# Two parts of a scan layer, instead of one and a half, computed between the experts of the layer before

## The chip, the cores and the metric

The kernel runs on one core of a Trainium2 chip. The metric is device time in microseconds (us) of one execution: the median of several runs. Engines are named as in the profile: PE (TensorE matmul) and PEld (its weight loads), DVE (VectorE), ACT (ScalarE), POOL (GpSimd), SP (SyncE, which here only issues DMAs).

## What is computed

Two transformer layers on x of 16 x 256 x 128 (batch, tokens, features) in float32, each with an attention-like half and a feed-forward half; both halves have a layer norm with a shift and a scale before them and a gate after them.

Layer 0: attention with 16 heads, then 16 experts (gate and up 128 to 256, down 128 to 128), all of them computed for every token and weighted by the scores of the router's best four. Layer 1: first the part that this change concerns,

```
k_real, v = x @ Wk, x @ Wv                    # 1024 columns: 16 heads of 64
k = exp(1j * 10 * k_real);  rotors = exp(1j * t * freqs)
out_pos   = real(cumsum_t(v * rotors)          * conj(rotors)) / sqrt(t + 1)
out_assoc = real(cumsum_t(v * conj(k_shifted)) * k)            / sqrt(t + 1)
y = (out_pos * g_pos + out_assoc * g_assoc) @ Wo
```

and then a small feed-forward half of three 128 x 128 matrices, called the mix below. With real numbers each cumulative sum is a cosine and a sine half (index `s`); `k` in the code is the batch element within a pair.

## The kernel before

The batch is taken in eight chunks (`NCH`) of two batch elements. Three stages follow one another, each with its instructions in an order written out by hand: on each engine they run in the order in which the program issues them.

**Attention of layer 0**, until about 302 us: not touched.

**The experts of layer 0**, about 302 to 690 us. The loop runs over n = 16 * chunk + e, so a step is one expert on one chunk. In a step PE makes three 128 x 512 products of two passes each: gate `pg` (L808) and up `pup` (L810) for n, and down into `acc` (L833) for n - 3. DVE adds bias to the gate (`g`, L812) and forms `u` for n - 1 (L824); ACT does `u` and the silu (L814, L817); POOL clamps `u` (L818) and multiplies it by the scores (`wide`, L825). Other work of a chunk is laid into fixed steps: the end of the old chunk at e = 2 to 4, the figures of the next layer norm on ACT at 5 and 6, its spread on POOL at 7 (L228, L229), the turning of the scores at 7. Generators that are advanced by one `next` per step put in more: `last_end` (router of the last chunk), `prepare` (the weights and rotors of layer 1, then `first_steps`), and `parts_ahead`.

`parts_ahead(c)` is what the change is about. The 1024 columns of the scan layer are eight parts j of 128 (`NJ`). For the first six chunks (`AHEAD` = 6) some of this is computed here, ahead of time, since layer 1 of a chunk can begin as soon as its layer 0 is through. It starts at e = 8 of the following chunk and computes, for chunk c, part 7 wholly (both sums) and of part 6 the position sum only. The work comes in pieces of 128 x 256, one for each (part, sum, k, s): POOL multiplies the values by the rotor or phasor (`bind`, L957), and in the next step DVE scans the product (L961), multiplies it by gate and probe (L965) and adds it to the total (L967), unless it is the first of its total. There are 12 pieces for a chunk, in steps 1 to 16 except 4, 7, 11 and 16. The two totals go to DRAM (L1007). Values and keys come from PE (L944, L979), their phases and sines from DVE (L985) and ACT (L983 to L989). PSUM pool `p_m` has one buffer for all of these.

**The scan layer and the mix**, from about 690 us. `PARTS` is the number of parts left for this stage: 7 for each of the first six chunks, 8 for the last two, so 58 steps. Part 6 of each of the first six chunks (`is_half`) has only its second sum to do here. In step n:

- DVE: scan of the assoc sum (`sum_assoc`, L1238) and of the position sum (`mem`, L1238), phases of n + 2 (`off`, L1213), `m_pos` (L1450), then parts of the mix and of the residual stream.
- POOL: read-out of the assoc sum of n - 1 (`sum_assoc`, L1456), then the two products to be scanned in n + 1 (`bound_pos`, `bound_assoc`, L1235).
- PE: assoc read-out of n - 1 into `pout` (L1252), mix matmuls, keys and values of n + 3 (L1197, L1201), position read-out of n (L1252).
- ACT: two sines and an absolute value for n + 2 (L1219 to L1221), the copies of keys and values out of PSUM (L1198, L1202), then parts of the mix.

A half step has one scan of two halves, one bound product, a read-out of which DVE takes one half (L1448) and POOL the other, and no `m_pos`.

`pout` has one PSUM buffer, so the first position read-out of a chunk waits until ACT's `gated_out` (L1277, oT) has read the old chunk's sum. The totals computed ahead are fetched at j = 1 (L1264) and enter `pout` by one matmul each (L1268): part 7 at j = 3, part 6 in the half step. The mix of chunk m is laid out by `place`, the number of steps since chunk m + 1 began, so that it spans the following chunks: means at 2, figures at 3, spread (POOL) at 4, norm at 5, `mix_tokens` at 6, the matmuls at 7, 8 and 9, the gating at 10 and 11, the output of the two batch elements at 12 and 13. With seven steps to a chunk, place 6 falls on the last step j = 6 and place 7 on j = 0 of the next chunk.

Of the kernel before, what the change touches and what calls it, by code (L numbers as in the profile page):

```python
# [11 lines left out]
F32 = mybir.dt.float32  # L12
# [6 lines left out]
P = 128  # L19
# [23 lines left out]

PARTS = [NJ - 1 if c < AHEAD else NJ for c in range(NCH)]
# [11 lines left out]
def tile_adaln_two_layers(ctx: ExitStack, tc: tile.TileContext, a: dict, out: bass.AP):  # L56
# [206 lines left out]
    with ExitStack() as moe_scope:  # L263
# [523 lines left out]
        with ExitStack() as scope:  # L787
# [141 lines left out]
            def parts_ahead(c):  # L929

# [7 lines left out]

                def values(j):
                    v = cross.tile([P, 2, T], F32, tag="o", name=f"v_ahead_{c}_{j}")
                    pv = p_m.tile([P, 2, T], F32, tag="m", name=f"pv0_{c}_{j}")
                    nc.tensor.matmul(pv, w_v1[:, ts(j, P)], flat, start=True, stop=True)  # L944
                    nc.scalar.copy(v, pv)
                    return v

                yield
                vs = {j: values(j)}
# [5 lines left out]
                def bind(q, nm, k, s, by):  # L955
                    t = cross.tile([P, T], F32, tag=("heads", "y")[s], name=f"bound_ahead_{nm}_{c}_{q}_{k}_{s}")
                    nc.gpsimd.tensor_tensor(t, vs[q][:, k, :], by, ALU.mult)  # L957
                    bound[q, nm, k, s] = t

                def read(q, nm, k, s, i, probe):  # L960
# [3 lines left out]
                    gate = gates[:, q, i : i + 1]  # L964
                    nc.vector.scalar_tensor_tensor(row if more else dst, row, gate, probe, ALU.mult, ALU.mult)  # L965
                    if more:
                        nc.vector.tensor_tensor(dst, row, dst, ALU.add)  # L967
                    written.add((q, k))

                cs = late.tile([P, 2, 2, T + 1], F32, tag="phasor_ahead", name=f"phasor_ahead_{c}")  # L970
                nc.gpsimd.memset(cs[:, :, :, 0:1], 0.0)
                assoc = [(j, "assoc", k, s, 1, cs[:, s, k, 0:T], cs[:, s, k, 1:]) for k in range(2) for s in range(2)]
                pos_, pos_before = (
                    [(q, "pos", k, s, 0, rotor[:, q, s, :], rotor[:, q, s, :]) for k in range(2) for s in range(2)]
                    for q in (j, j - 1)
                )
                yield
                pk = p_m.tile([P, 2, T], F32, tag="m", name=f"pk0_{c}")
                nc.tensor.matmul(pk, w_k1[:, ts(j, P)], flat, start=True, stop=True)  # L979
                off, size = (  # L980
                    cross.tile([P, 2, T], F32, tag="hn4", name=f"{nm}_ahead_{c}") for nm in ("off", "size")
                )
                nc.scalar.activation(off, pk, AF.Copy, bias=ROUND)  # L983
                yield
                nc.vector.scalar_tensor_tensor(off, off, ROUND, pk, ALU.subtract, ALU.subtract)  # L985
                nc.scalar.activation(size, off, AF.Abs)
                nc.scalar.activation(cs[:, 1, :, 1:], off, AF.Sin, scale=-TWO_PI_IN)
                yield
                nc.scalar.activation(cs[:, 0, :, 1:], size, AF.Sin, bias=half_pi, scale=-TWO_PI_IN)  # L989
                yield  # L990

                pieces = assoc + pos_ + pos_before
                late_one = None
                for step in range(1, NE + 1):
                    yield
                    if late_one:
                        read(*late_one[:5], late_one[6])
                        late_one = None
                    if step == 5:
                        vs[j - 1] = values(j - 1)  # L1000

                    if step not in (4, 7, 11, NE):
                        late_one = pieces.pop(0)
                        bind(*late_one[:4], late_one[5])
                assert not pieces and not late_one
# [3 lines left out]
            def past_others(steps=1):  # L1009

                while any((at["step"] + i) % NE in (3, 5, 7, *range(10, 16)) for i in range(steps)):
                    yield
# [154 lines left out]
    with ExitStack() as scope:  # L1167
# [55 lines left out]
        def is_half(n):  # L1223

            return steps[n][0] < AHEAD and steps[n][1] == NJ - 2

# [3 lines left out]
        def binders(n):  # L1230
            w = work[n]
            v2 = w["v"].unsqueeze(1).to_broadcast(both)
            for nm, bind in (("pos", rot(n)), ("assoc", phasor[n % 3][:, :, :, 0:T]))[is_half(n) :]:
# [3 lines left out]
        def summed(n, nm, dst, half=slice(0, 2)):  # L1237
            nc.vector.tensor_tensor_scan(  # L1238
                dst[:, half].rearrange("p s k t -> p (s k t)"),
                keep.rearrange("p (s k) t -> p s k t", k=2)[:, half].rearrange("p s k t -> p (s k t)"),  # L1240
                work[n][nm][:, half].rearrange("p s k t -> p (s k t)"),
# [176 lines left out]
        for n in range(last + 2):  # L1418
# [3 lines left out]
            place = {n - begin[m + 1]: m for m in (c - 2, c - 1) if 0 <= m < NCH - 1 and n <= last}  # L1422
# [5 lines left out]
            if j == 4 and AHEAD <= c + 1 < NCH:  # L1428
                into_tokens(c + 1, pt_tokens)
            if n <= last:  # L1430
                half = is_half(n)
                mem = p_mem.tile(both, F32, tag="mem", name=f"mem_{n}")
                if not half:
                    m_pos = hp.tile(both, F32, tag="m_pos", name=f"m_pos_{n}")
                m_assoc = hp.tile(both, F32, tag="sum_assoc", name=f"sum_assoc_{n}", bufs=3)
                work[n]["m"] = m_assoc
                if half:

                    summed(n, "assoc", mem, slice(0, 1))
                    summed(n, "assoc", m_assoc, slice(1, 2))  # L1440
                elif n:
# [217 lines left out]
```

## Time and profile before

| | us |
|---|---|
| median of 3 runs | 1080.41 |
| lowest, highest | 1078.15, 1080.94 |
| the profiled execution's own time | 1078.81 |
| its span (first to last instruction) | 1076.7 |

| stage | about, us | steps |
|---|---|---|
| attention of layer 0 | 0 to 302 | |
| experts of layer 0 | 302 to 690 | 128 |
| scan layer and mix | 690 to 1053, end of the last chunk to 1074 | 58 |

The granted TensorE clock is at full speed in all 40 slices of the page. A line of a stretch gives its bounds and length in us, then the busy time (and the number of instructions) of PE, PEld, DVE, ACT and POOL, then granted clock, busy share of the DMA engines and GB/s. A line of a timeline gives start and duration, engine, source line, operation, what is written and read, and in brackets how long the engine had stood idle and for what. A line of a group gives in addition the number of instructions, their busy time and the mean duration in ns. Durations overlap the next instruction's by some 0.05 us, so a sum of times goes by starts. Matmuls show 0.59 us each but start 0.43 us apart.

### The profile page before, as it was taken

Reading aid. Unit: us, or ns where it says so; the run is one execution under the profiler, and the core shown is the slowest. Engines: PE = TensorE matmul, PEld = TensorE weight load, DVE = VectorE, ACT = ScalarE, POOL = GpSimd, SP = SyncE. Lnnn points to the kernel's source line nnn. Section 1 sums busy time; section 2 is a strip of 40 time slices with the busy share of each in tenths; the row PEclk is TensorE's granted clock in tenths of the full one; section 3 lists DMA queues with packets and bytes.
Section 4 is the critical chain, followed back from the end, with each engine's and each line's share of the span. In section 5 each row is a group of like instructions: output and inputs, shape, how many; then the busy total and the mean of one; then the engine's idle time right before and its main releaser. Section 6 shows DMA issues by size and latency. Waiting matters only on the chain.

```text
span 1076.7 us, 16224 instructions
## 1 busy us (share of the span) xinstructions
PE 1020.6 (95%) x5333; PEld 517.4 (48%) x5333; DVE 912.8 (85%) x1413; ACT 704.4 (65%) x1515; POOL 796.8 (74%) x754
## 2 busy tenths in 40 slices
PE   7999999999999999999999999898999999999987
PEld 5566666676654444444444434333344444444334
DVE  6679878998756798988878788999999999999995
ACT  3776677667656676687767755365676767767662
POOL 2245334533557678888878788899999999999992
PEclk9999999999999999999999999999999999999999
DMA  3102100000052222322322232100000000000000
GB/s 117 43 11 69 50 8 3 2 4 2 4 178 98 80 99 79 118 101 96 109 89 89 89 101 95 59 10 10 20 3 27 15 15 30 1 11 5 5 10 19
DMA packets 35538, 53.15 MB, mean 49 GB/s; under 512 B 8416, under 2 KB 23296, under 8 KB 35456
## 3 DMA queue, kind: packets, MB, share of 16 engines
q1 hardware_dynamic: 34912, 51.87, 14.9%
q8 instruction: 42, 0.69, 0.3%
q14 instruction: 40, 0.33, 0.1%
q10 hardware_dynamic: 544, 0.26, 0.1%
HBM read 46.34 MB, written 5.51 MB: 48 GB/s over the span
## 4 chain that ended last, share of the span: by engine, by line
PE 53%; POOL 20%; DVE 11%; ACT 8%; issue 6%; DMA 1%; SPq 0%; DVEq 0%; POOLq 0%; ACTq 0%
PE pg L808 6%; PE acc L833 6%; PE pup L810 6%; PE s L440 5%; PE st L474 5%; PE po L494 5%; PE pout L1252 4%; POOL bound_assoc L1235 4%; POOL sum_assoc L1456 4%; POOL bound_pos L1235 4%; POOL u L825 3%; DVE mem L1238 2%; DVE sum_assoc L1238 2%; PE pq L567 2%; PE pk L1197 1%
## 5 line engine op out<-in xcount | busy, mean ns | idle before, releaser
L482 ACT ACTIVATE exp<-st 128x512 f32<-128x512 f32 x256 | 132.2, 603 | 85.9 <-PE st L474 85.9
L452 DVE TENSOR_REDUCE maxima<-s 128x2 f32<-128x512 f32 x256 | 158.8, 683 | 25.9 <-PE s L440 25.6
L825 POOL TENSOR_TENSOR u<-u,wide 128x512 f32<-128x512 f32 x128 | 164.6, 1286 | 16.5 <-DVE u L824 7.4
L833 PE MATMUL acc<-u,w_dn 128*128 128x512 f32 x256 | 133.9, 605 | 6.1 <-POOL u L825 5.9
L1238 DVE TENSOR_TENSOR_SCAN sum_assoc<-keep,bound_assoc 128x1024 f32<-128x1024 bf16 (+1 forms) x58 | 125.8, 2168 | 12.8 <-POOL bound_assoc L1235 12.8
L808 PE MATMUL pg<-hT,w_gu 128*128 128x512 f32 x256 | 131.9, 597 | 0.8 <-DVE logits L674 0.4
L810 PE MATMUL pup<-hT,w_gu 128*128 128x512 f32 x256 | 130.7, 592 | 0.0
L814 ACT ACTIVATE u<-pup,b_gu 128x512 f32<-128x512 f32 x128 | 87.0, 680 | 63.6 <-PE pup L810 57.6
L1235 POOL TENSOR_TENSOR bound_assoc<-v,phasor 128x1024 f32<-128x1024 f32 x57 | 124.9, 2192 | 0.2 <-ACT phasor L1221 0.2
L818 POOL TENSOR_SCALAR u<-u 128x512 f32<-128x512 f32 x128 | 80.3, 628 | 59.6 <-ACT u L814 53.4
L812 DVE TENSOR_SCALAR g<-pg,b_gu 128x512 f32<-128x512 f32 x128 | 95.3, 745 | 32.7 <-PE pg L808 32.4
L1456 POOL TENSOR_TENSOR sum_assoc<-sum_assoc,phasor 128x1024 f32<-128x1024 f32 (+1 forms) x58 | 121.5, 2094 | 0.4 <-DVE sum_assoc L1238 0.3
L1238 DVE TENSOR_TENSOR_SCAN mem<-keep,bound_pos 128x1024 f32<-128x1024 bf16 x52 | 118.1, 2271 | 0.0
L1235 POOL TENSOR_TENSOR bound_pos<-v,rotor 128x1024 f32<-128x1024 f32 x51 | 111.7, 2189 | 0.0
L1252 PE MATMUL pout<-sum_assoc,w_assoc 128*128 128x512 f32 x228 | 108.1, 596 | 3.6 <-POOL sum_assoc L1456 3.6
L1252 PE MATMUL pout<-m_pos,w_pos 128*128 128x512 f32 x204 | 97.2, 599 | 15.0 <-ACT oT L1277 12.0
L817 ACT ACTIVATE pg<-g 128x512 f32<-128x512 f32 x128 | 76.3, 596 | 42.3 <-DVE g L812 41.9
L824 DVE SCALAR_TENSOR_TENSOR u<-u,pg 128x512 f32<-128x512 f32 x128 | 86.7, 677 | 11.9 <-POOL u L818 9.9
L1219 ACT ACTIVATE phasor<-off 128x512 f32<-128x512 f32 x56 | 35.1, 627 | 78.3 <-DVE off L1213 78.3
L474 PE MATMUL st<-qx,kx 32*128 32x256 f32 x1024 | 81.7, 387 | 1.2 <-DMA qx<-turned 1.1
L833 PEld LDWEIGHTS acc<-u,w_dn 128*128 128x128 f32 x256 | 46.7, 191 | 74.3 <-issue 42.9
L440 PE MATMUL s<-kx,qx 32*128 32x256 f32 x1024 | 78.1, 407 | 4.2 <-DVE kx L577 1.8
(301 smaller groups left out, 1910.0 us busy)
## 6 DMA issues: line engine op xcount, KB each, us to landing
wide<-scores SPq DMA_DIRECT2D x64, 512.0 KB
qx<-turned SPq DMA_DIRECT2D x256, 1.0 KB
there<-total SPq DMA_DIRECT2D x12, 256.0 KB
fetched<-there SPq DMA_DIRECT2D x12, 256.0 KB
w_gu<-in_gate_up_dram SPq DMA_DIRECT2D x8, 256.0 KB
out_dram<-x SPq DMA_DIRECT2D x16, 128.0 KB
x<-in_x_dram SPq DMA_DIRECT2D x14, 128.0 KB
w_dn<-in_down_dram SPq DMA_DIRECT2D x4, 256.0 KB
```

What stands on the lines that cost most here:

```text
L440: nc.tensor.matmul(s[g][:, i, :], qs[c][r][rows_, k, ts(i, P)], ks[c][rows_, r // NS, k, :], start=True, stop=True,)
L452: nc.vector.tensor_reduce(mx[:, :, g], s[g], AX.X, ALU.max, negate=True)
L474: nc.tensor.matmul(st[g][:, i, :], ks[c][rows_, r // NS, k, ts(i, P)], qs[c][r][rows_, k, :], start=True, stop=True,)
L482: nc.scalar.activation(e[:, g, :, :], st[g], AF.Exp, scale=QSCALE)
L808: nc.tensor.matmul(pg, w_gu[:, e, 0 : 2 * D : 2], h2, start=True, stop=True)
L810: nc.tensor.matmul(pu, w_gu[:, e, 1 : 2 * D : 2], h2, start=True, stop=True)
L825: nc.gpsimd.tensor_tensor(u, u, wide[n // SOME][:, n % SOME, :], ALU.mult)
L833: nc.tensor.matmul(accs[c], w_dn[:, e, :], work.pop(n), start=False, stop=(e == NE - 1))
L1235: nc.gpsimd.tensor_tensor(w[nm], v2, bind, ALU.mult)
L1238: nc.vector.tensor_tensor_scan(dst[:, half].rearrange("p s k t -> p (s k t)"), keep.rearrange("p (s k) t -> p s k t", k=2)[:, half].rearra ...
L1252: nc.tensor.matmul(pos[c], w[:, j, :], m[:, k, :, :].rearrange("p k t -> p (k t)"), start=(j == 0 and i == 0 and k == 0), stop=(c < NCH - ...
L1456: nc.gpsimd.tensor_tensor(m[:, part], m[:, part], phasor[(n - 1) % 3][:, part, :, 1:], ALU.mult)
```

## The change

`PARTS` is 6 for each of the first six chunks: parts 6 and 7 are both done wholly between the experts, in 16 pieces to a chunk, and the half step with `is_half` is gone from the last stage, which has 52 steps. The pieces follow one another without a gap, one in each step, from step 15 on (counted so that step 16 is e = 0 of the next chunk): part 7 first, then part 6, each with its position sum first. Values, keys, phases and sines of part 6 are new and have steps of their own; those of part 7 are moved. Of the 12 additions to totals for a chunk, four (the second assoc half of each total) are done by POOL, from an SBUF tile into which DVE writes its product; the other eight stay on DVE.

In the last stage, mix places are looked up three chunks back (13 places of 6-step chunks reach into a third chunk); the spread on POOL moves from the end of place 4 to place 5, between the read-out and the two products; place 13's output is joined to place 12's; the fetched totals enter at j = 3 (part 6) and j = 4 (part 7); the tokens of chunks 6 and 7 are turned one step earlier. The steps at which `first_steps` may put its own work are changed to fit.

```diff
-PARTS = [NJ - 1 if c < AHEAD else NJ for c in range(NCH)]
+PARTS = [NJ - 2 if c < AHEAD else NJ for c in range(NCH)]
...
+                def values(q):
...
+                def keys(q):
+                    pk = p_m.tile([P, 2, T], F32, tag="m", name=f"pk0_{c}_{q}")
+                    nc.tensor.matmul(pk, w_k1[:, ts(q, P)], flat, start=True, stop=True)
+                    off = cross.tile([P, 2, T], F32, tag="hn4", name=f"off_ahead_{c}_{q}")
+                    nc.scalar.activation(off, pk, AF.Copy, bias=ROUND)
+                    offs[q] = pk, off
+
+                def phases(q):
+                    pk, off = offs[q]
+                    nc.vector.scalar_tensor_tensor(off, off, ROUND, pk, ALU.subtract, ALU.subtract)
+
+                def sines(q):
+                    pk, off = offs.pop(q)
+                    cs = late.tile([P, 2, 2, T + 1], F32, tag="phasor_ahead", name=f"phasor_ahead_{c}_{q}")
+                    nc.gpsimd.memset(cs[:, :, :, 0:1], 0.0)
+                    size = cross.tile([P, 2, T], F32, tag="hn4", name=f"size_ahead_{c}_{q}")
+                    nc.scalar.activation(size, off, AF.Abs)
+                    nc.scalar.activation(cs[:, 1, :, 1:], off, AF.Sin, scale=-TWO_PI_IN)
+                    nc.scalar.activation(cs[:, 0, :, 1:], size, AF.Sin, bias=half_pi, scale=-TWO_PI_IN)
+                    css[q] = cs
...
-                def read(q, nm, k, s, i, probe):
+                def read(q, nm, k, s):
+                    probe = rotor[:, q, s, :] if nm == "pos" else css[q][:, s, k, 1:]
                     nc.vector.tensor_tensor_scan(row, keep_all, bound.pop((q, nm, k, s)), 0.0, ALU.mult, ALU.add)
                     dst = sum_of[q][:, k, :]
                     more = (q, k) in written
-                    gate = gates[:, q, i : i + 1]
-                    nc.vector.scalar_tensor_tensor(row if more else dst, row, gate, probe, ALU.mult, ALU.mult)
+                    by_pool = nm == "assoc" and s
+                    t = row if more else dst
+                    if by_pool:
+                        t = cross.tile([P, T], F32, tag="oT", name=f"read_ahead_{c}_{q}_{k}")
+                    i = 0 if nm == "pos" else 1
+                    nc.vector.scalar_tensor_tensor(t, row, gates[:, q, i : i + 1], probe, ALU.mult, ALU.mult)
                     if more:
-                        nc.vector.tensor_tensor(dst, row, dst, ALU.add)
+                        (nc.gpsimd if by_pool else nc.vector).tensor_tensor(dst, t, dst, ALU.add)
                     written.add((q, k))
...
+                pieces = [
+                    (q, nm, k, s) for q in (j, j - 1) for nm in ("pos", "assoc") for k in range(2) for s in range(2)
+                ]
                 late_one = None
-                for step in range(1, NE + 1):
-                    yield
+                for step in range(12, 2 * NE + 16):
+                    yield
+                    if step == 12:
+                        values(j)
+                    if step == 14:
+                        keys(j)
+                    if step == 15:
+                        phases(j)
+                    if step == NE:
+                        sines(j)
+                    if step == NE + 5:
+                        values(j - 1)
+                    if step == NE + 8:
+                        keys(j - 1)
+                    if step == NE + 9:
+                        phases(j - 1)
+                        sines(j - 1)
                     if late_one:
-                        read(*late_one[:5], late_one[6])
+                        read(*late_one)
                         late_one = None
-                    if step == 5:
-                        vs[j - 1] = values(j - 1)
-
-                    if step not in (4, 7, 11, NE):
+                    if step >= 15 and pieces:
                         late_one = pieces.pop(0)
-                        bind(*late_one[:4], late_one[5])
-                assert not pieces and not late_one
+                        bind(*late_one)
+                    if not pieces and not late_one:
+                        break
...
-                while any((at["step"] + i) % NE in (3, 5, 7, *range(10, 16)) for i in range(steps)):
+                while any((at["step"] + i) % NE in (3, 5, 7, 8, 10, 12, 14) for i in range(steps)):
...
-            place = {n - begin[m + 1]: m for m in (c - 2, c - 1) if 0 <= m < NCH - 1 and n <= last}
+            place = {n - begin[m + 1]: m for m in (c - 3, c - 2, c - 1) if 0 <= m < NCH - 1 and n <= last}
...
-            if j == 4 and AHEAD <= c + 1 < NCH:
+            if j == 3 and AHEAD <= c + 1 < NCH:
                 into_tokens(c + 1, pt_tokens)
...
+            if 5 in place:
+                mix_spread(place[5], hp)
             if n + 1 <= last:
                 binders(n + 1)
...
-                if j == 3 and c < AHEAD:
-                    with_fetched(c, NJ - 1, w_last[:, 1])
+                if j in (3, 4) and c < AHEAD:
+                    with_fetched(c, NJ - 5 + j, w_last[:, j - 3])
...
-            if 4 in place:
-                mix_spread(place[4], hp)
...
-            for k in range(2):
-                if 12 + k in place:
-                    mix_out(2 * place[12 + k] + k, py[:, k])
+            if 12 in place:
+                for k in range(2):
+                    mix_out(2 * place[12] + k, py[:, k])
```

## The prediction

> **What bounds the kernel now.** I read part 1 of the page, then the busy time of each engine in stretches cut at chunk borders, the timelines inside one chunk of each stage, and last the chain over a chunk.
>
> ```profile
> PE 1020.6 (95%) x5333; PEld 517.4 (48%) x5333; DVE 912.8 (85%) x1413; ACT 704.4 (65%) x1515; POOL 796.8 (74%) x754
> 443.00:489.10 46.10, 46.10 (x117) 20.78 (x116) 41.48 (x73) 35.78 (x83) 39.88 (x47) 1.00 0.29 102
> 489.10:536.40 47.30, 47.30 (x120) 21.34 (x119) 38.70 (x68) 36.64 (x88) 39.25 (x48) 1.00 0.31 102
> 814.10:857.90 43.80, 41.94 (x107) 18.80 (x106) 42.43 (x37) 30.62 (x67) 43.00 (x23) 1.00 0.06 19
> ```
>
> The first line hides two stages. The other three show PE, PEld, DVE, ACT and POOL busy. Between the experts (302 to 690 us) PE never idles in a whole chunk and the others have 10 to 24% to spare; the chain of 443 to 489 is PE alone. In the last stage (690 to 1053) POOL, DVE and PE are all within 2 us of the period, 43.8 us per chunk (the half part's scan starts at 814.11 and again at 857.92).
>
> ```profile
> 819.30 2.29 DVE L1238 TENSOR_TENSOR_SCAN sum_assoc<-keep,bound_assoc 128x1024 f32<-128x1024 bf16 x1 [1.37 <-POOL bound_assoc L1235]
> ...
> 828.26 1.98 PE L1252 MATMUL pout<-m_pos,w_pos 128*128 128x512 f32 x4 [1.86 <-ACT oT L1277]
> ...
> 851.10 1.01 POOL L228 TENSOR_TENSOR rstd_f<-off_f,neg_half 128x4 f32<-128x4 f32 x1 [0.72 <-ACT off_f L221]
> ```
>
> These are the only waits of each engine in that chunk. POOL's starts lie 2.13 us apart (820.45, 822.58, 824.72), so a whole part costs it 6.4, the half part 2.13 + 1.23 = 3.36, the spread 1.24: 38.4 + 3.36 + 1.24 + 0.72 of waiting = 43.7. So **POOL sets the last stage and PE the stage between the experts**.
>
> **The change, last stage.** Six half parts go. Each took 3.36 us of POOL, 3.42 of DVE (814.11 to 817.53), and on PE keys, values and two read-outs, 4 x 0.86 = 3.43. Its ACT work (3.0 us) has no price: ACT is busy 30.6 of 43.8. The spread is now queued on POOL behind the read-out of step 5, two steps after its figures on ACT, so the wait of 0.72 goes as well (chunk 0 has none). What is left per chunk: POOL 38.4 + 1.24 = 39.6; DVE 6 x 6.10 + 1.03 + 4 x 0.33 = 38.9; PE 41.94 - 3.43 = 38.5, plus its wait for oT.
>
> That wait is what is late next. With six steps to a chunk, `mix_tokens` falls on step j = 0, on ACT ahead of `gated_out`. PE's `pout` of the new chunk is queued behind oT, and keys, values and DVE's phases behind that. Its two instructions take 1.03 us (L254 at 820.88). If PE is the late one: from the end of the old chunk's last read-out, transposes 0.44, keys and values 1.72, then on ACT the copy of the values, done 0.63 after PE is through with them, tokens 1.0, oT 0.85: PE stands 2.5 us, and a chunk takes 38.5 + 2.5 = 41.0. Now DVE needs ACT's copy of the keys 1.0 to 3.5 us after it is there (copy ends 835.6, phases start 836.9), and the mixes move so that keys at j = 2 come some 1.9 later: PE's lag can't hide wholly. Bounds for chunks 2 to 5: 39.6 (POOL alone) and 42 (41.0 and one more us for ACT, whose sigmoid 1.7 and figures 2.1 now share step 3 with its 3.0 of every step). I take 40.7, near PE's sum. Gain: chunk 0 3.4, chunk 1 (no mixes on PE until its end) 4.2, chunks 2 to 5 4 x 3.1 = 12.4: **20.0 us**, bounds 7.6 + 4 x 1.8 = 14.8 and 7.6 + 4 x 4.2 = 24.4. Two outputs sent in one step, the fetched parts entering at steps 3 and 4 and the tokens of chunks 6 and 7 a step earlier cost nothing: the same matmuls, additions and DMAs one step aside (DMA busy share 0.06 there).
>
> **The change, between the experts.** For each of six chunks there are 16 pieces instead of 12, one in every step.
>
> ```profile
> L979 PE MATMUL pk<-hT,w_k 128*128 128x512 f32 x12 | 6.4, 614 | 1.7 <-ACT v_ahead L945 1.7
> L957 POOL TENSOR_TENSOR und_ahead_pos<-v_ahead,rotor 128x256 f32<-128x256 f32 x48 | 33.2, 692 | 0.0
> L967 DVE TENSOR_TENSOR total<-sums,total 128x256 f32<-128x256 f32 x48 | 20.4, 424 | 1.6
> L664 POOL TENSOR_TENSOR x<-x,y 128x256 f32<-128x256 f32 x16 | 11.6, 726 | 9.7 <-DVE y L662 8.8
> ...
> 492.70 0.70 DVE L961 TENSOR_TENSOR_SCAN sums<-sums,und_ahead_pos 128x256 f32<-128x256 f32 x1 [0.81 <-POOL und_ahead_pos L957]
> 493.44 0.49 DVE L965 SCALAR_TENSOR_TENSOR sums<-sums,gates,rotor 128x256 f32<-128x256 f32 x1
> 493.96 0.42 DVE L967 TENSOR_TENSOR total<-sums,total 128x256 f32<-128x256 f32 x1
> 494.30 0.74 DVE L812 TENSOR_SCALAR g<-pg,b_gu 128x512 f32<-128x512 f32 x1
> 494.96 0.68 DVE L824 SCALAR_TENSOR_TENSOR u<-u,pg 128x512 f32<-128x512 f32 x1
> 495.56 0.74 DVE L812 TENSOR_SCALAR g<-pg,b_gu 128x512 f32<-128x512 f32 x1
> ```
>
> PE: the second part's keys, two passes at 0.43, 0.86 x 6 = **5.2 us**, all on the path. Keys now follow values by two steps, so the 1.7 us in the first line goes. ACT: one more offset, size and two sines, 2.5 us a chunk beside 36 of 47: hidden. DVE: by the last six lines a step with a piece and an addition takes 2.86 us (492.70 to 495.56), without it 2.40. New per chunk: 4 scans with their products and one set of phases; the additions stay 8. POOL: clamp 0.6, product with the weights 1.25, bind 0.67 = 2.52 per step; new per chunk 4 binds and 4 additions. The addition on POOL has no row in this place; L664, same shape, gives 0.70 from start to start; bounds 0.42 (DVE's L967) and 1.25 (the 512-wide product). In it POOL waits for DVE's product of the same step; behind it stand the next bind, clamp and product, and for those PE's `acc`. DVE's product ends about 4.5 us after the step's `pg`, POOL gets there at 5 to 6: no wait.
>
> Sum of a plain chunk: PE 46.4 (starts of `pg` at 488.6 and 535.0) + 0.86 = 47.3; DVE 16 steps = 42.3 + 1.2 phases + 0.75 = 44.3; POOL 16 x 2.52 + 4 x 0.70 + 1.2 + 0.2 = 44.5. PE stays the longest by 6%, but the queues touch. Where PE has only its three matmuls (2.58 us a step) and pieces come each step, the last chunk runs slower: `pg` starts at 667.99, 670.72, 673.53, 676.38, 679.06, 2.77 a step. After the change four such steps stand together (15, 0, 1, 2): 4 x 0.19 = 0.8. At step 7, where `acc` already comes 0.05 to 0.15 after POOL's u, the spread meets a bind and an addition, 1.37 more on POOL, of which PE's new keys at step 8 give back 0.86: 0.5. That is 1.3 x 5 chunks = 6.5. In the last chunk seven such steps (9 to 15) cost 1.3 where four cost 0.7 now: 0.6. **Between the experts: +5.2 - 1.7 + 7.1 = +10.6 us**; bounds +3.5 (no new waits) and +18 (pieces at 3.2 us a step; the third rival). The stores to DRAM go out one step earlier on SP; what is queued behind (`wide`, four steps ahead) has waited for POOL longer already.
>
> GPSIMD Engine Reference, section Engine selection, of the Trainium skill speaks against the third on POOL: a two-input elementwise operation is about twice as slow there as on VectorE. The rows here say 726 against 424 ns, 1.7 times; by the page the 24 additions would take 20.4 instead of 16.8 us of POOL, an estimate. Perfetto Trace Analysis, section Identifying the Most-Contended Engine, says that matmul busy time is no good measure and LDWEIGHTS busy is, which is 45% here; by it TensorE had room, the keys were free, and the time 5.2 lower. But 0.43 from pass to pass is never undercut in either stage.
>
> **Sum.** 1078.8 (profiled execution: span 1076.7, 2.1 around it) - 20.0 + 10.6 = 1069.4. That execution lies 1.6 under the median 1080.4; on the median's scale it is 1071.0.
>
> **Rivals.** (A) PE's lag hides in the last stage and POOL sets 39.6. For: PE has slack in chunks 0, 1, 6, 7. Against: the 1.0 us margins. 1080.4 - 24.4 + 10.6 = 1066.6. (B) The mixes bunched on steps 0 to 3 make 42 a chunk: 1080.4 - 14.8 + 10.6 = 1076.2. For: PE has 29 us in those four steps, POOL 25.6. (C) Slower: between the experts DVE and POOL, not PE, set the pace, through the loop bind, scan, product, g, u, weights, POOL addition, bind (0.67 + 0.74 + 0.54 + 0.66 + 0.60 + 1.25 + 0.70 = 5.2 per two steps, before clamps, spreads, phases and stream additions in between). From step 31 to 127 a step now takes 3.00 us ((679.06 - 390.7) / 96); beyond 3.21 the gain of 20 is gone. At 3.3 it is + 28.8 - 20.0: 1089. For: three engines over 94%; chunks 2 and 6 also carry the rotors and first steps. Against: 2.77. That the half parts don't go can't be: the list of steps has 52 entries instead of 58.
>
> **Numbers.** Forecast 1071.0 (1067.5 to 1074) 0.43; A 0.20; B 0.17, half of it faster by over 0.3%; C 0.15; between B and C 0.05. 0.3% (3.2 us) is about what can be told from no change. Faster 0.72, same 0.13, slower 0.15. Range: 1080.4 - 24.4 + 3.5 = 1060 to 1080.4 - 14.8 + 18 = 1084.
>
> **What would show it.** Starts of the first scan at j = 0 40 to 41 us apart in chunks 2 to 5; PE's wait for oT near 2.5 or more; no wait at L228. Between the experts `pg` starts some 48 us apart per chunk, PE busy over 96%, `acc` waiting for POOL's u more than the 4.3 us of now. I am wrong if that stage grows by more than 18 us, or if the period stays above 42.

## The result, and the profile after

The changed kernel takes 1087.01 us (median of 6 runs, 1086.12 to 1088.57) beside 1080.59 us for the kernel before on the same chip. The ratio on record is 1.0066, 95% interval [1.0048, 1.0083]; that of the two medians is 1.0059. So it is slower by 0.6 to 0.7% where a gain, 1071.0, was forecast, and 1087.0 lies above the range of 1060 to 1084.

The profiled execution has a span of 1086.6 us. I cut each span at the first `pg` and at the `pg` of step 127:

| | attention | experts, 127 steps | the rest | span |
|---|---|---|---|---|
| before | 302.0 | 377.1 | 397.6 | 1076.7 |
| after | 303.9 | 402.1 | 380.6 | 1086.6 |
| difference | +1.9 | **+25.0** | **-17.0** | +9.9 |

The attention stage has no changed instruction; its start of the experts lies between 301.4 and 303.9 us in all profiles of this case. The last stage gained nearly what was forecast (20.0). Most of the error lies between the experts: +25.0 instead of +10.6. PE's idle time in that stage rose from 6.7 to 19.2 us.

First part 1 of the page after:

```profile
PE 1016.1 (94%) x5297; PEld 514.2 (47%) x5297; DVE 924.7 (85%) x1443; ACT 702.4 (65%) x1510; POOL 809.2 (74%) x796
```

Then three stretches of it: two chunks between the experts (4 and 5) and one of the last stage (columns as in the section on the profile before).

```profile
499.20:548.80 49.60, 48.06 (x119) 21.10 (x118) 43.31 (x76) 39.11 (x92) 44.40 (x58) 1.00 0.27 96
548.80:603.70 54.90, 49.99 (x123) 21.96 (x122) 47.12 (x83) 34.05 (x74) 49.30 (x65) 0.99 0.27 97
846.40:887.20 40.80, 38.49 (x98) 17.43 (x98) 39.34 (x33) 28.03 (x63) 39.63 (x21) 1.00 0.06 20
```

Between the experts PE, which had no idle time in the two chunks shown before, idles 1.5 and 4.9 us in these two, and no other engine has filled the time: DVE has 6 and 8 us to spare, POOL 5 and 6. So what is new there isn't an engine that is full, but waits, and slow passes behind some of them. In the last stage the chunk shown takes 40.8 (40.7 forecast).

Per chunk (16 steps, from `pg` to `pg`) the stage between the experts went from 48.9, 46.5, 46.4, 50.3, 49.8 us in chunks 2 to 6 to 53.2, 50.8, 49.6, 54.9, 54.2, and the 15 steps of chunk 7 from 44.0 to 48.1. Taken step by step, four places carry most of it.

**1. The keys of the first steps (chunks 5 and 6, step 15).** The timeline of PE, then of DVE, then two stretches, all of the kernel after:

```profile
602.47 1.44 PE L1047 MATMUL pk<-hT,w_k 128*128 128x512 f32 x2 [2.82 <-DVE off_ahead L960]
603.70 1.91 PE L807 MATMUL pg<-hT,w_gu 128*128 128x512 f32 x2
```

```profile
601.33 0.48 DVE L988 SCALAR_TENSOR_TENSOR read_ahead<-sums,gates,phasor_ahead 128x256 f32<-128x256 f32 x1
601.73 0.68 DVE L960 SCALAR_TENSOR_TENSOR off_ahead<-off_ahead,pk 128x512 f32<-128x512 f32 x1
```

```profile
600.00:603.00 3.00, 0.54 (x2) 0.30 (x2) 2.38 (x5) 0.60 (x1) 2.83 (x4) 1.00 0.53 175
603.00:606.00 3.00, 3.00 (x5) 1.20 (x4) 0.35 (x1) 0.60 (x1) 0.76 (x2) 0.52 0.23 87
```

The pool `p_m` has one buffer. The keys of part 7, moved to step 14, hold it until DVE has made their phases, at the end of its step 15. The change lets `first_steps` put its own keys (L1047) into that very step 15, ahead of `pg`, and PE runs in order: all of it stands for 2.82 us. Then the granted clock is 0.52 for 3 us, the two passes of `pg` start 0.85 apart instead of 0.43. Steps 95 and 111 take 6.79 and 6.59 us instead of 2.57: +8.2 us in two steps.

**2. A third table load on ACT (chunk 2, steps 0 to 4).** ACT's table loads there, before and after, with what stands between them:

```profile
396.60 1.28 ACT L319 ACT_TABLE_LOAD   x1
397.89 0.47 ACT L319 ACTIVATE rt_exp<-rt_exp 128x320 f32<-128x320 f32 x1
398.96 1.28 ACT L817 ACT_TABLE_LOAD   x1
```

```profile
398.38 1.28 ACT L318 ACT_TABLE_LOAD   x1
399.67 0.47 ACT L318 ACTIVATE rt_exp<-rt_exp 128x320 f32<-128x320 f32 x1
400.05 0.61 ACT L967 ACTIVATE size_ahead<-off_ahead 128x512 f32<-128x512 f32 x1
400.68 1.28 ACT L968 ACT_TABLE_LOAD   x1
401.98 0.63 ACT L968 ACTIVATE phasor_ahead<-off_ahead 128x512 f32<-128x512 f32 x1
402.51 0.71 ACT L969 ACTIVATE phasor_ahead<-size_ahead,half_pi 128x512 f32<-128x512 f32 x1
403.81 1.28 ACT L816 ACT_TABLE_LOAD   x1
```

The first chunk's sines of part 7, moved to step 0, fall between the router's exponential and the next silu. One switch of tables more, and 2 us of sines, hold up the silu and ACT's `o` (L841); PE waits 2.11 us for it (at 407.09), and the clock falls again. Steps 3 and 4 of chunk 2 cost +3.3 and +0.8.

**3. Part 6's keys at step 8 (chunks 2 to 4).** They share the buffer with the turned scores of step 7. PE, then ACT, after:

```profile
526.86 1.12 PE L953 MATMUL pk<-hT,w_k 128*128 128x512 f32 x2 [1.09 <-ACT scT L340]
```

```profile
526.24 0.57 ACT L340 ACTIVATE scT<-psc 16x512 f32<-16x512 f32 x1
```

Step 8 is longer by 1.21, 1.70 and 2.23 us, of which the keys themselves are 0.86.

**4. Step 10 (chunks 2 to 4 and 7).** +1.48, +0.85, +0.79, +1.63: `acc` waits for POOL's u. In chunk 4:

```profile
532.60 1.12 PE L832 MATMUL acc<-u,w_dn 128*128 128x512 f32 x2 [0.32 <-POOL u L824]
```

POOL is late since step 7, where the spread, an addition and a bind stand in a row, and has no pause from there to step 10.

In the last stage two waits were forecast, one to grow and one to go. PE and POOL, after:

```profile
847.24 1.99 PE L1265 MATMUL pout<-m_pos,w_pos 128*128 128x512 f32 x4 [2.33 <-ACT oT L1290]
```

```profile
872.22 1.01 POOL L227 TENSOR_TENSOR rstd_f<-off_f,neg_half 128x4 f32<-128x4 f32 x1 [1.09 <-ACT off_f L220]
```

PE's wait for oT is 2.33 us in four chunks (2.5 forecast). The wait ahead of the spread should have gone; it is 1.09 to 1.69 in five chunks where it was 0.71 to 0.93.

### The profile page after: what moved, and what is told of

The parts are those of the page before. It is cut to its first block, busy times and chain, and to the rows that moved or that the text cites. A ratio compares the mean times of both kernels' runs of the same rounds, so it can differ in the third digit from the quotient of the medians.

```text
span 1086.6 us, 16211 instructions
## 1 busy us (share of the span) xinstructions
PE 1016.1 (94%) x5297; PEld 514.2 (47%) x5297; DVE 924.7 (85%) x1443; ACT 702.4 (65%) x1510; POOL 809.2 (74%) x796
## 4 chain that ended last, share of the span: by engine, by line
PE 52%; POOL 19%; DVE 14%; issue 7%; ACT 5%; DMA 1%; SPq 0%; DVEq 0%; POOLq 0%; ACTq 0%
PE pout L1265 9%; POOL u L824 6%; PE s L439 5%; PE st L473 5%; PE po L493 5%; PE pg L807 4%; PE pup L809 3%; PE acc L832 3%; POOL bound_pos L1248 3%; DVE sums L980 2%; PE pv L1218 2%; PE pk L1214 2%; POOL bound_assoc L1248 2%; POOL sum_assoc L1458 2%; POOL u L817 2%
## 5 line engine op out<-in xcount | busy, mean ns | idle before, releaser
L807 PE MATMUL pg<-hT,w_gu 128*128 128x512 f32 x256 | 134.4, 607 | 1.4 <-DVE u L823 0.7
L1251 DVE TENSOR_TENSOR_SCAN sum_assoc<-keep,bound_assoc 128x1024 f32<-128x1024 bf16 x52 | 118.8, 2285 | 10.7 <-POOL bound_assoc L1248 10.6
L1265 PE MATMUL pout<-m_pos,w_pos 128*128 128x512 f32 x204 | 100.2, 615 | 18.1 <-ACT oT L1290 15.3
L1458 POOL TENSOR_TENSOR sum_assoc<-sum_assoc,phasor 128x1024 f32<-128x1024 f32 x52 | 113.7, 2186 | 0.3 <-DVE sum_assoc L1251 0.3
L1248 POOL TENSOR_TENSOR bound_assoc<-v,phasor 128x1024 f32<-128x1024 f32 x51 | 111.6, 2189 | 1.0 <-ACT phasor L1238 1.0
L1265 PE MATMUL pout<-sum_assoc,w_assoc 128*128 128x512 f32 x204 | 96.9, 597 | 3.6 <-POOL sum_assoc L1458 3.6
L809 PEld LDWEIGHTS pup<-hT,w_gu 128*128 128x128 f32 x256 | 50.9, 199 | 61.4 <-issue 50.8
```

Of the source, the lines that this page charges most:

```text
L807: nc.tensor.matmul(pg, w_gu[:, e, 0 : 2 * D : 2], h2, start=True, stop=True)
L809: nc.tensor.matmul(pu, w_gu[:, e, 1 : 2 * D : 2], h2, start=True, stop=True)
L1248: nc.gpsimd.tensor_tensor(w[nm], v2, bind, ALU.mult)
L1251: nc.vector.tensor_tensor_scan(dst.rearrange("p s k t -> p (s k t)"), keep.rearrange("p s t -> p (s t)"), work[n][nm].rearrange("p s k t - ...
L1265: nc.tensor.matmul(pos[c], w[:, j, :], m[:, k, :, :].rearrange("p k t -> p (k t)"), start=(j == 0 and i == 0 and k == 0), stop=(c < NCH - ...
L1458: nc.gpsimd.tensor_tensor(m, m, phasor[(n - 1) % 3][:, :, :, 1:], ALU.mult)
```

## The experiments

Unless said otherwise each kernel is the one after with the edit shown. "Experts" and "rest" are the two parts of its profiled span, as above; the ratio is to the kernel before, run on the same chip.

| | median, us | ratio and interval | experts | rest |
|---|---|---|---|---|
| before | 1080.6 | | 377.1 | 397.6 |
| after | 1087.0 | 1.0066 [1.0048, 1.0083] | 402.1 | 380.6 |
| 1 first keys out of steps 9, 15 | 1075.2 | 0.9959 [0.9940, 0.9978] | 391.9 | 379.8 |
| 2 all sines of part 7 a step later | 1085.9 | 1.0055 [1.0040, 1.0071] | 400.2 | 378.8 |
| 3 all additions on DVE | 1081.5 | 1.0018 [1.0004, 1.0033] | 397.4 | 381.2 |
| 4 only the last stage changed | 1061.4 | 0.9823 [0.9803, 0.9842] | 377.2 | 380.4 |
| 5 = 1, chunk 0's sines later | 1076.9 | 0.9963 [0.9949, 0.9977] | 392.2 | 382.9 |
| 6 = 1, other additions on POOL | 1082.0 | 1.0012 [0.9997, 1.0027] | 392.9 | 385.0 |
| 7 = 1, gating first | 1071.0 | 0.9906 [0.9889, 0.9923] | 391.9 | 373.8 |
| 8 = 1, figures first | 1081.4 | 1.0007 [0.9991, 1.0023] | 391.9 | 384.8 |
| 9 keys of part 6 at step 1 | 1080.6 | 1.0003 [0.9992, 1.0015] | 393.0 | 382.0 |
| 10 = 7 and 3 | 1065.8 | 0.9866 [0.9846, 0.9886] | 389.4 | 372.7 |
| 11 = 10 and 9 | 1064.8 | 0.9858 [0.9838, 0.9878] | 388.0 | 371.8 |
| 12 before, gating first | 1074.1 | 0.9946 [0.9925, 0.9966] | 377.1 | 393.2 |

**Experiment 1: the collision alone.**

```diff
-                while any((at["step"] + i) % NE in (3, 5, 7, 8, 10, 12, 14) for i in range(steps)):
+                while any((at["step"] + i) % NE in (3, 5, 7, 8, 9, 10, 12, 14, 15) for i in range(steps)):
```

> Only the steps in which the generator of the first two scan steps may put its matmuls are changed: 9 and 15, in which the one PSUM buffer is still held by keys of a part ahead, are barred too. Theory A (collisions): in the changed kernel the keys of the first steps stand at step 15 behind that buffer, PE idles 2.8 us twice and then runs 1.7 us worth at half clock, 4.2 and 4.0 us in steps 95 and 111. Both go: 7 to 8.5 us less than the changed kernel, about 1079. Theory B (the loop of DVE and POOL sets the pace between the experts, PE's waits are only where the slack shows): less than 2 us.

It took 1.07% off (11.6 us by the two ratios), more than either theory gave: from slower than before to faster than before, by one condition of a generator. Steps 95 and 111 lose 4.21 and 4.01, and PE at the same place shows:

```profile
599.08 1.02 PE L832 MATMUL acc<-u,w_dn 128*128 128x512 f32 x2
600.38 1.13 PE L1047 MATMUL pk<-hT,w_k 128*128 128x512 f32 x2 [0.27 <-DVE off_ahead L960]
601.34 1.02 PE L807 MATMUL pg<-hT,w_gu 128*128 128x512 f32 x2
```

The keys still wait for the same phases, but a step later, 0.27 us, and at full clock. Of the 10.2 us that the stage loses, 8.2 are these two steps; the rest lies in other steps of chunks 6 and 7, as the edit also moves what the generator does next.

**Experiments 2 and 5: the third table load.** Experiment 2 moves `sines(j)` from step NE to NE + 1 for all chunks, experiment 5 (on experiment 1) for the first chunk alone, as shown:

```diff
-                    if step == NE:
+                    if step == (NE if c else NE + 1):
```

> Only the sines of part 7 go one step later (e = 1 instead of 0). Theory A: in chunk 2 they stand directly behind the router's exponential, so that ACT loads three tables in steps 32 to 34 instead of two (1.28 us each) and PE stands 2.1 us and loses 1.7 us to the clock; one load fewer and no stall: 2 to 4 us less, steps 35 and 36 back to 4.3 and 2.6 us. Theory B: no change beyond 1 us.

> Experiment 1 (no keys of the first steps at steps 9 and 15) with the sines of part 7 of the first chunk alone put one step later, behind the step in which the router's Exp is issued. Theory A (the third table load of chunk 2 stands on the path): steps 35 and 36 lose most of their 4.0 us over the kernel before and no other chunk changes; 1071 to 1073 against some 1075 for experiment 1. Theory B (the load is hidden, the time of steps 35 and 36 comes from the sines themselves, wherever they stand): within 1 us of experiment 1, and chunk 2 as long as there (some 53.2 us).

The load is gone in both. In experiment 5 steps 3 and 4 of chunk 2 are 2.35 and 0.76 shorter than after, but step 8 is 1.45 longer: of the 4.0, 1.5 stays gained there. In experiment 2 the other chunks give it back, +1.1 to +2.2 at step 3, as the later sines hold up ACT's `o`; its median is 1.1 below the kernel after, where theory A expected 2 to 4, and its profile is that of the shortest of its ten executions. Theory A holds for the load, not for its price; experiment 5's 1076.9 lies outside the ranges of both of its theories. That its profile isn't below experiment 1's comes from three other places, at which PE waited as long but the clock was lower (below): 1.7 us in chunk 5, 1.5 at the handover to the last stage, 1.7 at the first long wait for oT.

**Experiments 3 and 6: the additions on POOL.** Experiment 3, and then experiment 6 (on experiment 1), which takes the other half, in steps without the spread:

```diff
-                    by_pool = nm == "assoc" and s
+                    by_pool = False
```

```diff
-                    by_pool = nm == "assoc" and s
+                    by_pool = nm == "assoc" and not s
```

> The four additions per chunk go back from POOL to DVE, nothing else. Theory A: POOL's u is late at step 7 and in the last chunk partly because of them; the last chunk's steps 119 to 127 (25.9 us) come 1 to 2 us shorter, other chunks under 0.5 each: 1 to 4 us less in all. Theory B: 5 us or more less if POOL's share sets the loop, or as much more if DVE's does.

> Experiment 1 with POOL's four additions per chunk moved from the second half of each phasor pair to the first (steps 4, 6, 12, 14 in place of 5, 7, 13, 15), none of them thus in the step of the spread's product. Theory A (the additions cost where POOL's u is late for the step's reading product, at step 10 above all): the 0.7 to 1.1 us at step 10 of each chunk goes, 1 to 5 us in all, 1070 to 1074. Theory B (POOL's hold-up is the sum of its work over the chunk, wherever an addition stands): within 1.5 us of experiment 1's 1075.

The groups of the addition in the kernel after, on DVE and on POOL:

```profile
L990 DVE TENSOR_TENSOR total<-sums,total 128x256 f32<-128x256 f32 x48 | 20.4, 425 | 1.6
L990 POOL TENSOR_TENSOR total<-read_ahead,total 128x256 f32<-128x256 f32 x24 | 17.4, 727 | 0.2
```

With all 72 on DVE the experts' stage is 4.7 shorter and the median 5.5, more in all than theory A's 1 to 4; the end of the last chunk gives 1.1, as theory A said. On top of experiment 7, experiment 10 gains 5.2 in the median, but only 2.6 in this stage. Step 10 loses 0.7 to 1.1 in four chunks. Moving the additions away from the spread (experiment 6) gives 0.9 and 0.7 of this in chunks 2 and 4 and loses more at steps 0 to 4: experts 392.9 against experiment 1's 391.9, which in this stage is theory B. The median, 1082.0, lies 5 us above the nearer of the two ranges; the profile shows the difference behind this stage (see the clock, below). So the price isn't that of the one step with the spread; that it is POOL's load through the chunk which makes u late for `acc` fits this, but isn't shown by itself.

**Experiment 4: the last stage alone.** The part ahead is that of the kernel before (12 pieces), the last stage that after; the assoc sum of part 6 is left out for six chunks. The main lines:

```diff
-                pieces = [
-                    (q, nm, k, s) for q in (j, j - 1) for nm in ("pos", "assoc") for k in range(2) for s in range(2)
-                ]
+                pieces = assoc + pos_ + pos_before
...
```

> The last stage of the changed kernel with the 12 pieces of the kernel before between the experts; the assoc sum of part 6 is left out for six chunks. If the two stages add up, the time is that of before less the 17.0 us by which the last stage is shorter in the changed kernel's trace: 1063 to 1065. If the last stage depends on how the experts end (DVE's and POOL's queues), 1066 or more.

Experts 377.2, rest 380.4: each stage has the length it has in the kernel it comes from. The two halves of the change add up, and no work runs over from one into the other. The median, 1061.4, is 1.6 below the range; the profiled spans differ by 17.6, close to the 17.0, and the rest isn't explained by them.

**Experiments 7, 8 and 12: what sets the last stage.** All three move lines only: experiments 7 (on experiment 1) and 12 (on the kernel before) the gating `gated_out`, which makes oT, experiment 8 (on experiment 1) the figures. In the code both are on ACT: what the expectations call a division on VectorE is this gating on ScalarE, and the wait behind the spread that they put on VectorE is POOL's, ahead of L227.

```diff
+            if j == 0 and c:
+                o = gated_out(c - 1)
             if 7 in place and n < last:
                 mixed(place[7], wk_now, wk_before, "pk2")
...
-            if j == 0 and c:
-                o = gated_out(c - 1)
```

```diff
+            if 3 in place:
+                mix_figures(place[3], hp)
             if 9 in place:
                 mix_sigmoid(place[9])
...
-            if 3 in place:
-                mix_figures(place[3], hp)
```

> Experiment 1 with, in the last stage, the division by the norm that makes the next chunk's operand (oT) issued on VectorE before the cosines of that step instead of behind them and the token turn. Theory A (PE's wait of 1.4 to 2.8 us for oT in each chunk sets part of the stage's pace): the six waits vanish and the stage after step 127 falls from some 381 by 6 to 12 us, 1064 to 1070. Theory B (VectorE's own work is what fills a chunk's 41 us, PE only waits because it is ahead): the wait vanishes or moves to another matmul, the stage changes by less than 2 us, 1073 to 1077.

> Experiment 1 with, in step 3 of the last stage, the norm's figures issued on ScalarE before the sigmoid of that step. Theory A (the 1.1 to 1.7 us for which VectorE stands still behind the spread, 6.3 us in five chunks, is ScalarE's sigmoid ahead of the figures): these waits fall below 0.8 each and the stage loses 2 to 6 us, 1069 to 1073. Theory B (the wait is ScalarE's whole queue at that place, and what is later on it, above all the step's offset for the phases, is what VectorE waits for next): the wait moves, less than 1.5 us of change, 1073.5 to 1077.

> The kernel before with the same move of the division ahead of the cosines, and nothing of the change. It tells whether the gain of that move belongs to the change. Theory A (in the kernel before the 1.86 us for which PE waits for oT is on the path in the same way): the last stage of 397.6 us falls by 4 to 9 us, 1072 to 1077. Theory B (before, the part without position matmuls gives the time back: VectorE's and POOL's half steps set the chunk's 43.8 us): less than 2 us, 1079 to 1082.

With the gating first, PE's waits for oT are gone and the rest falls by 5.9 against experiment 1: theory A, just under its lower edge (the median, 1071.0, is 1 us above its range). A chunk then takes 39.7. Experiment 11 has the same last stage; one chunk of it, and POOL around the spread:

```profile
826.40:866.10 39.70, 38.79 (x99) 17.55 (x98) 39.05 (x33) 27.50 (x63) 39.62 (x21) 1.00 0.07 21
```

```profile
850.75 2.16 POOL L1459 TENSOR_TENSOR sum_assoc<-sum_assoc,phasor 128x1024 f32<-128x1024 f32 x1
852.88 1.00 POOL L227 TENSOR_TENSOR rstd_f<-off_f,neg_half 128x4 f32<-128x4 f32 x1
853.96 0.20 POOL L228 TENSOR_TENSOR less_f<-less_f,rstd_f 128x4 f32<-128x4 f32 x1
```

POOL is busy 39.62 of 39.70 us and doesn't wait for the spread: the bound of rival A, 39.6, is reached.

With the figures ahead of the sigmoid (experiment 8) POOL's wait at the spread is gone too, but a chunk takes 41.05 instead of 40.82. POOL and DVE, experiment 8:

```profile
857.21 2.18 POOL L1248 TENSOR_TENSOR bound_assoc<-v,phasor 128x1024 f32<-128x1024 f32 x1 [1.01 <-ACT phasor L1238]
```

```profile
862.66 0.42 DVE L1352 TENSOR_TENSOR r<-pv,r 128x256 f32<-128x256 f32 x1 [2.03 <-ACT r L1341]
```

The wait moved to a sine and to the sigmoid behind it, as theory B said. But the rest is 5.0 longer than in experiment 1, and the median, 1081.4, lies 4 us above theory B's range. In the profile 4.8 of the 5.0 are passes at a low clock, 1.5 to 1.7 each at the handover and at the waits for oT at 795.54 and 920.34; without them theory B's size holds too. All ten executions are above six of the seven of experiment 1; why this order meets more of these drops isn't shown.

Experiment 12 shows that the gain of the gating isn't the change's: before, it gives 0.54% (5.8 us; 4.4 in the rest of the profiled span), theory A.

**Experiment 9, and the sums 10 and 11.** In experiment 9 the steps from which `first_steps` keeps out are (1, 2, 3, 5, 7, 10, 12, 14, 15), to fit:

```diff
-                    if step == NE + 8:
+                    if step == NE + 1:
                         keys(j - 1)
-                    if step == NE + 9:
+                    if step == NE + 2:
                         phases(j - 1)
+                    if step == NE + 9:
                         sines(j - 1)
```

> The changed kernel with the keys of part 6 at step 1 and their phases at step 2 of the next chunk, in place of 8 and 9; the sines stay at 9, and the keys of the first steps keep out of the steps around both keys, so that experiment 1's gain (10 to 12 us) should be in it. Theory A (at step 8 PE waits for the one pair of banks until ScalarE has copied the token turn: 0.35, 0.84 and 1.37 us in chunks 2 to 4): step 8 falls back to 2.58, step 1 rises by the 0.86 of the two matmuls, net -0.3 to -1.4 a chunk against experiment 1, 1070 to 1075. Theory B (the wait goes along with the keys, as the pair of banks is held by whatever comes ahead of them at step 1 as well): step 1 rises by more than 0.86, the time is within 1.5 us of experiment 1's, 1074 to 1077.

> Experiment 7 with experiment 3's additions: the keys of the first steps out of steps 9 and 15, the last stage's division ahead of the cosines, all additions between the experts on VectorE. If the three causes are separate, their sum holds: experiment 7's 1071.0 less 4 to 5.5 us, 1065 to 1067. If POOL's additions and the collisions of experiment 1 were the same time (both are lateness of the loop of VectorE and POOL), less: 1068 to 1071.

> The same with the keys of part 6 at step 1 (experiment 9). If experiment 9's theory A holds: 1 to 4 us below the kernel with additions on VectorE and the division first, 1062 to 1066. If its theory B holds: no difference to it above 1.5 us.

In experiment 9 step 8 loses 1.21, 1.51 and 2.22 in chunks 2 to 4, step 1 gains 0.86 and step 10 another 0.96 and 1.29 in chunks 3 and 4: with the keys away, `acc` reaches POOL's late u sooner (in chunk 4 it waits 1.83 us there, 0.32 in the kernel after). Neither theory as written: the stage gains nothing (393.0 against experiment 1's 391.9), and the median, 1080.6, is above both ranges, 1.7 us of it by a low clock at the first long wait for oT. Experiment 10's median falls where separate causes would put it (1065.8; 1065 to 1067 expected), but the stage between the experts gives only 2.6 of experiment 3's 4.7, so the additions and the collisions were in part the same time, and the median's fit is in part luck. Experiment 11 is the best of all, 1.0 below it, at the lower edge of what theory A expected from the keys and within what theory B allows: the two aren't told apart. It beats the kernel before by 1.4%.

**The clock.** In the page's row PEclk a 9 stands for 90% or more, so 40 nines don't mean full speed throughout. The kernel before has a drop too, at its handover to the last stage, after waits of 1.30 and 1.60 us for POOL:

```profile
686.00:689.00 3.00, 3.00 (x4) 1.16 (x5) 2.52 (x6) 0.00 (x0) 1.59 (x2) 0.51 0.00 0
```

Experiments 1 and 5 have the same instructions at the first long wait for oT, and the same wait. PE there, and the stretch behind it, in experiment 1:

```profile
793.24 1.98 PE L1265 MATMUL pout<-m_pos,w_pos 128*128 128x512 f32 x4 [2.77 <-ACT oT L1290]
```

```profile
796.00:799.00 3.00, 3.00 (x9) 1.33 (x8) 3.00 (x5) 0.95 (x2) 3.00 (x3) 1.00 0.00 0
```

And in experiment 5:

```profile
795.44 3.63 PE L1265 MATMUL pout<-m_pos,w_pos 128*128 128x512 f32 x4 [2.77 <-ACT oT L1290]
```

```profile
796.00:799.00 3.00, 3.00 (x5) 1.00 (x4) 2.16 (x3) 1.81 (x3) 3.00 (x3) 0.54 0.00 0
```

After 2.77 us of waiting the clock stays at 1.00 in one execution and falls to 0.54 in the other, where the four passes take 1.65 us more. So such a wait is priced once in itself and in some executions a second time. The first collision can be split in the same way, as experiment 2 has it unchanged at step 95, but there the clock stays:

```profile
600.03 1.12 PE L1047 MATMUL pk<-hT,w_k 128*128 128x512 f32 x2 [2.86 <-DVE off_ahead L960]
601.00:604.00 3.00, 3.00 (x9) 1.36 (x8) 1.95 (x4) 1.63 (x3) 0.59 (x2) 1.00 0.23 87
```

Steps 95 and 96 together take 6.0 us before, 10.8 after, 9.1 in experiment 2 and 6.6 in experiment 1. Of the 4.2 us that experiment 1 takes away there, 1.7 is clock and the rest waiting.

The profiled execution of experiment 6 is 5.3 us longer in the rest than that of experiment 1: 1.7 at this step, and 3.6 in the handover from step 127, where PE waits 1.61, 1.52 and 2.29 us for POOL (0.74 and 2.20 in experiment 1), the first keys of the last stage stand one `acc` later on PE, and the clock is 0.77 and 0.54 over 10 us. Experiments 5, 8 and 9 lose the same 1.6 to 1.7 at this step. Medians that lie some us apart are therefore read here together with their spans' parts. It isn't plain chance from one execution to the next: the mean clock lies between 0.990 and 0.993 in all seven executions of experiment 1, between 0.984 and 0.990 in all twenty of experiments 6 and 8.

## Why the prediction was wrong, point by point

- **What bounds each stage**: right for the kernel before. In the last stage POOL is the bound once the waits are gone (experiment 11: 39.6 of 39.7 us). Between the experts PE stayed the busiest engine, but what the change added there is 12.6 us of idle time on PE and 12.4 of busy time, and only 5.2 of the latter are its new passes: being the longest by 6% kept no wait away. (DVE's sum was a little low: by the starts of the lines shown a step without an addition takes 2.52 us, not 2.40, so 45.0 and not 44.3; PE stays the longest.)
- **Last stage, -20.0**: measured -17.0, inside the bounds of 14.8 and 24.4. Right in its mechanism: 40.8 a chunk for 40.7 in chunks 3 and 4, PE late by 2.33 us for oT for 2.5. By the starts of the first scans chunk 0 gains 5.3 (3.4 forecast), chunk 1 2.1 (4.2), chunks 2 and 5 1.9 and 2.6 (3.1 each; chunk 2 with a clock loss), and chunk 6 loses 1.3, which wasn't priced.
- **"So the wait of 0.72 goes as well"**: wrong. POOL's wait at the spread grew to 1.09 to 1.69; the working itself put sigmoid and figures into one step of ACT and priced that only for PE. Rival A, in which PE's lag hides, needed another order (experiment 7) to come true, and then it came true to 0.1 us a chunk.
- **Keys of part 6 on PE, +5.2, and the wait of 1.7 that goes**: the two passes cost 0.86 at step 8, as said, and the wait went. That they share a buffer with the turned scores (0.35, 0.84, 1.37 more) was not priced.
- **"New waits", +7.1: the step that failed.** Measured +25.0 - 5.2 + 1.7 = +21.5. The term priced lean steps and step 7, the places where queues touch, and nothing that comes of other work of the same stage. Missing were: the keys of `first_steps` behind the moved keys in a pool with one buffer, with the clock that PE lost behind them, 10.2 us of this stage (experiment 1); the additions on POOL, priced as "no wait", 2.6 to 4.7 (experiments 10 and 3); the sines of the first chunk meeting the router's table, 4.0 in the trace, of which a later place saves 1.5 (experiment 5). The edit of `past_others` stands in the diff; the working doesn't mention it. Nor has it a term for a low clock, having read the row PEclk as full speed.
- **Signs**: the stage grew by more than the 18 us named as the sign of being wrong. `pg` starts 49.6 and 54.9 us apart in the two chunks shown, for some 48; `acc` waits 7.8 us for POOL's u by the page after, 5.9 by the page before.
- **Rival C, 1089**: nearest in its number, though the range ended at 1084 below it. A step did take 3.26 us from step 31 to 127 ((706.0 - 392.6) / 96), over the 3.21 that it named. Its mechanism, the loop of DVE and POOL, is the smaller part: taking the additions off POOL gives 5.5, moving two matmuls of PE by one step gives 11.6. That its number is near is luck.
- With the collisions and POOL's additions out (experiment 11) the experts' stage is 10.9 us longer than before, and +10.6 was forecast; against the kernel before with the same gating (experiment 12) the change is worth -9.3 us, and -9.4 was forecast. The sums agree, their places don't: chunks 2 to 4 carry 10.6 of the 10.9, chunks 5 to 7 next to nothing, while the forecast spread it evenly. This agreement is luck as well.

Open: what decides whether the clock falls after a wait of a given length. And no run shortened the wait at step 8 in all chunks without a longer one elsewhere.

## What to carry to other kernels

When a step is moved in a schedule written by hand, list all that shares its buffer, its table and its queue in the new place, generators with rules of their own included: an edit of such a rule is an edit of the order on the bottleneck engine. A buffer held from one engine's step to another's next step belongs in the sum like an instruction, and so does a function that needs another table between two that share one. And where TensorE is the bound, a new wait of some 2 us can cost slow passes besides itself, here about 1.7 us where the clock fell; the forecast's bounds should leave room for them.

## What the hardware showed

- **The clock falls after short waits, and not each time.** A wait of PE of 1.95 us (chunk 5, for the residual stream) was followed by a granted clock of 1.00 in the kernel after and 0.51 in experiment 5. The 2.77 us for oT cost clock in seven profiles of nine (not in experiments 1 and 2), the 2.33 us behind it in one of 32 (experiment 3: four passes in 3.60 us instead of 1.98), 2.47 us for `m_pos` near the end in eleven of twelve, the 1.85 us for oT never. The place counts, then, and not the length alone. The Trainium skill, TensorE: Matmul & The Clock Gate, section What's actually happening, gives an idle window of about 3.4 us that runs freely, so that the point of the change depends on where in the window the work falls. That the length alone doesn't decide agrees with these rows; the length given doesn't, as waits well below 3.4 us are already followed by half the clock here.
- **A switch of ACT's table costs 1.28 us and no more**: the load at 398.38 is followed by its exponential at 399.67.
